# A two-layer graph network: four buffers for W1's slots, and four steps asked for in other places of the plan

## The chip, the core and the metric

The kernel runs on one core of a Trainium2 chip. The metric is the device time of one launch in microseconds (us). The engines go by their short names: PE (TensorE, matmuls; PEld its weight loads), DVE (VectorE), ACT (ScalarE), POOL (GpSimd) and SP (SyncE, which here issues nearly all transfers, in order).

## What is computed

Two graph layers over 32 graphs ("batches") of 512 nodes with 512 features, all in float32. The reference, cut to its core:

```python
# layer 0, per batch
h   = relu(layernorm(x))
agg = (adj @ h) / maximum(sum(adj, -1), 1e-6)
x   = x + relu(concat([h, agg]) @ W.T)            # W: 512 x 1024
# layer 1
h   = relu(layernorm(x))
q, k = split(h @ Wqk); v = h @ Wv
agg = adj @ (k * mask)
w   = mask * sum(q * agg, -1) / sqrt(512)
x   = x + softmax(w)[:, None] * v
```

## The kernel before

**Strassen-like products.** Each product of two 512 x 512 matrices is split into 2 x 2 blocks of 256 and done with seven block products instead of eight. A matrix that takes part is held in seven "slots" (`[P, 7, 2, H]` with P = 128, H = 256): four blocks and three sums of them. `left_sums` and `right_sums` make the sums on DVE, four operations each. `product` (L118) runs the seven products in the order 1, 2, 6, 5, 7, 3, 4. It keeps three PSUM banks: `pp` (reused by five of the products), `pr` and `pq`. After a product the result goes out of PSUM, by a copy on ACT (`c11`, `c12`, `m5`, `c22`) or by an addition on DVE (`finish`). A product that reuses a bank waits for the copy out of it.

**Stages of a batch i.** They are written as Python generators that yield between groups of matmuls:

- Y (`layer0_y`, 7 steps): h times the second half of W.
- O (`layer0_out`, 14 steps): h times the first half of W (W1), then adj times Y, added in the same banks; the output adds to x.
- TV (`layer1_tv`, 14 steps): the second layer's two products with Wq Wk^T and Wv, kept as `ptv` banks and the tile `tv`, with one more level of splitting. It runs for batch i-1 behind O of batch i. The last batches run it in two separate halves (`layer1_one`, banks `pw`).
- U (`layer1_u`, 7 steps): adj times the masked h of layer 1.

The order in time is O(i), TV(i-1), U(i), Y(i+1), O(i+1), and so on. `start` does the first batch's Y and O with its own plan, and prepares the weights.

**The plan.** Everything that isn't a matmul of the running stage is put by hand at a step of it: `p.at(n, f)` calls f after the n-th group of matmuls has been written into PE's stream. `run` emits the stage and the plan together. Since every engine takes its instructions in order, this fixes the order on all of them. Code that a stage runs behind a yield, as a copy out of a bank, comes behind what the plan put at that step.

**The parts that the plan moves about.**

- `Stream` (L402): W1's seven slots are read from DRAM again in every batch, in the order of their use, into a ring of three buffers (`tag="w1"`, tile `w`, source `dw`). Three loads are put at step 0 of U, four at steps 1, 3, 5, 7 of O.
- `FrontH`: x of a later batch into two half tiles (tile `n`, two buffers, shared with adj's half tiles `a`), its statistics on DVE, the normalisation on ACT (`write`, which also sends it to DRAM, `dhT`), the reading back in blocks (`to.read`, tile `shT`) and the 32 x 32 transposition on DVE (`turn`, tile `wide`).
- `FrontA`: the same for adj: `sum` on ACT gives the row sums (`deg`), `degrees` on DVE their reciprocals, `write` on ACT scales the rows, `daT` and `saT` are its copies, `turn` writes `aT`.
- `FrontH1` and `Post`: the second layer's front (`h1m`, `dh1T`, `sh1T`, `h1T`), and its end: `recombine` and `dot` on DVE, the softmax over nodes (`scores`, `maximum` on POOL, `shift`, `exponents` on ACT, `row_sum`, `weights`), and `apply` on ACT, which scales the rows of `tv`.

The softmax of batch 30, the last but one, is in the plan of U of batch 31: `shift` and `exponents` at step 2, behind the turns and sums of `h1T`.

The identity matrix for PE's transposes is a constant tile of its own (L218). The mask is kept twice, once with the factor 1/sqrt(512) (`mcol`, used by `factor` at L339) and once without (`mraw`).

Of the kernel before, what the change touches and what calls it, by code (L numbers as in the profile page):

```python
# [11 lines left out]
F32 = mybir.dt.float32  # L12
AF = mybir.ActivationFunctionType
ALU = mybir.AluOpType
AX = mybir.AxisListType

P = 128
# [5 lines left out]
def kernel(  # L23
# [35 lines left out]
    nc = tc.nc  # L59
    B, N, F = x.shape  # L60
    C = N // P
    H = F // 2
# [3 lines left out]
    scale = 1.0 / math.sqrt(wqk.shape[1] // 2)  # L66

    const = ctx.enter_context(tc.tile_pool(name="const", bufs=1))
    big = ctx.enter_context(tc.tile_pool(name="big", bufs=1))
# [29 lines left out]
    def copy(o, i):  # L99
        nc.scalar.activation(o, i, AF.Copy)  # L100
# [114 lines left out]

    mhalf = const.tile([P, C], F32, name="mhalf")
    nc.vector.memset(mhalf, -0.5)
    identity = const.tile([P, P], F32, name="identity")  # L218
    make_identity(nc, identity)

    X, AT_, DEG, W, Y, H1M, H1T, U, TV = ({} for _ in range(9))

    def xu_tile(name):
        return big.tile([P, C * 512], F32, tag="xu", bufs=2, name=name)

    def load_x(b):
# [87 lines left out]
    class FrontA:  # L314
# [21 lines left out]

        def factor(self):
            W[self.b] = small.tile([P, C], F32, tag="wd", bufs=3, name=f"wd_{self.b}")
            nc.gpsimd.tensor_tensor(W[self.b], DEG[self.b], mcol[:, :, self.b], op=ALU.mult)  # L339

        def write(self, c):
            v = self.n[c // 2][:, c % 2, :]
# [59 lines left out]
    class Stream:  # L402
# [6 lines left out]

        def load(self):  # L410
            k = ORDER[self.n % 7]
            t = big.tile([P, 2, H], F32, tag="w1", bufs=3, name=f"w1_{self.n}")
            nc.sync.dma_start(out=t, in_=self.d[RIGHT[k]])
            self.tiles.append((k, t))
            self.n += 1
# [281 lines left out]
        else:  # L697
            nc.vector.transpose(dst[:, :, ts(h, H)].rearrange("p a (k r) -> p k a r", r=R), t)

    mcol = const.tile([P, C, B], F32, name="mcol")  # L700
    mraw = const.tile([P, C, B], F32, name="mraw")

    def in_order(t):
# [6 lines left out]
    held = {}  # L710

    def turn_chunk(src, c, name):

        p = held[name, c] = mm_tile(f"{name}_{c}").rearrange("p a f -> p (a f)")
        for k in range(C):
            nc.tensor.transpose(p[:, ts(k, P)], src[:, ts(k, P)], identity)

    def keep_chunk(dst, c, name, by=copy):
        by(
# [4 lines left out]
    FH, FA, F1 = {}, {}, {}  # L724
# [24 lines left out]

    def start():  # L750

        load_x(0)
        s2 = [exchange(weight_source(w0[:, F:2 * F])[8 * h:8 * h + 8], f"sw2_{h}") for h in range(2)]
        fa = FA[0] = FrontA(0)
# [9 lines left out]
        fh = FH[1] = FrontH(1)  # L764
# [1 line left out]
            fh.load(h, room[:, 9728 + 1024 * h:9728 + 1024 * (h + 1)].rearrange("p (c f) -> p c f", c=2))  # L766
        sq = exchange(weight_source(wqk[:, 0:F]), "swq", rows16(5632))
        sk = exchange(weight_source(wqk[:, F:2 * F]), "swk", rows16(7680))
        late = big.tile([P, 7, 7, P], F32, tag="h1T", bufs=1, name="late").rearrange("p s i f -> p (s i f)")
        wqT = late[:, 0:2048].rearrange("p (c f) -> p c f", c=C)  # L770
        wkT = late[:, 2048:4096].rearrange("p (c f) -> p c f", c=C)
        mask_sb, mask_by = late[:B, 4096:4608], late[:B, 4608:5120]
# [4 lines left out]
        t = norm_tiles("0_0")  # L777
# [31 lines left out]
        p = Plan()  # L809
# [22 lines left out]
        fb = FA[1] = FrontA(1)  # L832
        p = Plan()
# [13 lines left out]
        p.at(7, lambda: nc.sync.dma_start(out=stream.d.rearrange("s p b f -> p s (b f)"), in_=w1R.rearrange("p s b f -> p s (b f)")))  # L847
        for h in range(2):
            for c in range(2):
                p.at(7 + 3 * h + c, fb.sum, 2 * h + c)  # L850
                p.at([11, 12, 13, 13][2 * h + c], fb.write, 2 * h + c)
            p.at(9 + 3 * h, fb.degrees, h)
        p.at(7, turn_rows, sq[:, 0:8], 0, wqT, True)
        p.at(8, turn_rows, sq[:, 8:16], 1, wqT, True)
        p.at(9, turn_rows, sk[:, 0:8], 0, wkT, False)
# [10 lines left out]
                nc.tensor.transpose(m[:, c, :], mask_by[:, ts(c, P)], identity[:B, :B])  # L866

        def mask_keep():
            nc.scalar.activation(mcol, held["pmk"], AF.Copy, scale=scale)
            nc.scalar.activation(mraw, held["pmk"], AF.Copy)  # L870

        p.at(8, mask_order)
        f = F1[0] = FrontH1(0)
# [7 lines left out]
        p = Plan()  # L881
# [7 lines left out]
                )  # L889

        def place(d, which, src):
            copy(
                mv[:, 2 * (d // 2):2 * (d // 2) + 2, 2 * (d % 2):2 * (d % 2) + 2, which, :],
                src.rearrange("p (a b f) -> p a b f", a=2, b=2),
            )

        def outer(s):
# [31 lines left out]
    with tc.manual_schedule(engines=engines):  # L929
        weights, mvR = start()  # L930
        post = None
        for i in range(B):
# [3 lines left out]
            f = F1[i]  # L936
            if i > 0:

                p = Plan()
                for n in range(4):  # L940
                    p.at(2 * n + 1, stream.load)
                right_y = right_sums(of(Y[i]))
                p.at(0, right_y[0])
# [27 lines left out]
                    p.at(2 + k, f1.inner_sums, k, 0, 7)  # L971
                if 1 < i and i + 2 < B:
                    fh = FH[i + 2]
                    for c in range(C):
                        p.at(3 + c, fh.stats, c)
                        p.at(10 + c, fh.write, c)
                    p.at(7, variance, fh.t)
                    p.at(9, shift, fh.t)
                if more:
                    th = FH[i + 1]  # L980
                    p.at(2, th.to.read, 1)
                    p.at(11, th.turn, 0)
                if 1 < i and i + 2 < B:
                    fa = FA[i + 2] = FrontA(i + 2)
# [7 lines left out]
                post = Post(i - 1, F1[i - 1])  # L992
                p = Plan()
# [19 lines left out]
                if i == 1:  # L1013
# [3 lines left out]
                    fh = FH[3]  # L1017
# [29 lines left out]
            p = Plan()  # L1047
            if more:
                p.at(0, f.turn, 0)
                p.at(1, f.turn, 1)  # L1050
                p.at(2, FA[i + 1].to.read, 0)
                p.at(3, FA[i + 1].to.read, 1)
                for n in range(3):
                    p.at(0, stream.load)
            if i == 0:
                fh = FH[2]
                for c in range(C):
                    p.at(2 + c, fh.stats, c)
                p.at(5, variance, fh.t)
                p.at(6, shift, fh.t)  # L1060
                p.at(6, weights[0])
            elif more:
                for k in range(7):
                    p.at(1 + k // 4, post.recombine, k, 1, 0)
                for c in range(C):
                    p.at(3 + c // 2, post.dot, c)
                p.at(5, post.scores)
                p.at(5, post.maximum)
                if i == 1:
                    for c in range(C):  # L1070
                        p.at(3 + c, fa.sum, c)
                    p.at(5, fa.degrees, 0)
                elif i + 2 < B:
                    for c in range(C):
                        p.at(c, fa.write, c)
                if 1 < i and i + 3 < B:
                    FH[i + 3] = FrontH(i + 3)
                    p.at(6, FH[i + 3].load, 0)
            else:
                p.at(0, f.turn, 0)  # L1080
                p.at(1, f.turn, 1)
                s4 = big.tile([P, 8, P], F32, tag="s", bufs=2, name="s4")
                for k in range(4):
                    p.at(1, f.inner_sums, k, 0, 2, s4)
                for k in range(4):
                    p.at(2 + k // 2, f.sums, k)
                for k in range(4):
                    p.at(4 + k // 2, f.inner_sums, k, 2, 7, s4)
                p.at(2, post.shift)
                p.at(2, post.exponents)  # L1090
                p.at(3, post.row_sum)
                p.at(4, post.weights)
            run(layer1_u(i), 7, p)


            if more:
                p = Plan()
                fb = FA[i + 1]
                p.at(2, fb.turn, 0)
                p.at(3, fb.turn, 1)  # L1100
                p.at(4, fb.sums, 0)
                p.at(4, fb.sums, 2)
                p.at(1, load_x, i + 1)
                if i + 2 < B:
                    p.at(5, FH[i + 2].to.read, 0)
                if i > 0:
                    p.at(0, post.shift)
                    p.at(1, post.exponents)
                    p.at(2, post.row_sum)
                    p.at(4, post.weights)  # L1110
                    for k in range(7):
                        p.at(3 + k // 2, post.recombine, k, None, 1)
                p.at(2, FA[i].factor)
                if i == 0:
                    for c in range(C):
                        p.at([2, 3, 4, 4][c], fh.write, c)
                    for k in range(1, 4):
                        p.at(3 + k, weights[k])
                    FA[2] = FrontA(2)
                    p.at(5, FA[2].load, 0)  # L1120
                    p.at(6, FA[2].load, 1)
                elif i == 1:
                    p.at(0, fa.degrees, 1)
                    for c in range(C):
                        p.at(2 + c, fa.write, c)
                    FH[4] = FrontH(4)
                    p.at(5, FH[4].load, 0)
                    p.at(6, FH[4].load, 1)
                elif i + 3 < B:
                    p.at(0, FH[i + 3].load, 1)  # L1130
                run(layer0_y(i + 1), 7, p)

        final = Post(B - 1, F1[B - 1])
        p = Plan()
# [16 lines left out]
        p = Plan()  # L1151
# [48 lines left out]
```

## Time and profile before

| | us |
|---|---|
| median of 9 runs | 2281.8 |
| lowest, highest | 2280.61, 2284.58 |
| the profiled execution (one of the nine) | 2284.58 |
| its span, first to last instruction | 2282.5 |
| outside its span | 2.08 |

The profile page starts with the busy time of each engine, and then shows the span in 40 equal slices, a digit being the busy share of a slice in tenths:

```profile
PE   7998999999999999999999999999999999999998
PEld 6787888888888888888888888888888888888897
DVE  6787888888888888888888888888888888888778
ACT  4454434454444454345444344443444443445323
POOL 0000000000100000000000000001000000000000
PEclk9999999999999999999999999999999999999999
DMA  9977878787778878777878787787788787877553
```

PE is full in all slices but a few at the start, and in the last one; DVE follows it closely; ACT has room. PEclk is the clock granted to TensorE in tenths of full speed, a mean over 57 us here, so a short drop doesn't show. DMA is the mean busy share of the 16 DMA engines.

The transfers that the change touches are these (what, by which engine's queue, times, size of one, median us from issue to landing):

```profile
w<-dw SPq DMA_DIRECT2D x217, 256.0 KB, 4.2
...
sh1T<-dh1T SPq DMA_DIRECT2D x256, 128.0 KB, 3.4
shT<-dhT SPq DMA_DIRECT2D x248, 128.0 KB, 4.4
...
saT<-daT SPq DMA_DIRECT2D x248, 128.0 KB, 3.3
...
n<-in_x_dram SPq DMA_DIRECT2D x240, 128.0 KB, 3.6
```

In the rows of the prediction a time stamp counts from the span's start. A row gives the start, the length, the engine, the line, the operation, what it writes and reads, and in square brackets the idle time before it and what ended that. Two rows of a pipelined engine overlap, so distances between starts are the measure. The line of a helper (L130 is the matmul of `product`, L100 the copy, L94 the addition, L97 the subtraction) stands for many uses; the names of the tiles tell them apart.

### The profile page before, as it was taken

The numbers are of one execution on the slowest core, as the hardware profiler recorded it, in microseconds if no ns is written. First come the engines' busy times: TensorE is split into PE (matmuls) and PEld (weight loads), VectorE is DVE, ScalarE is ACT, GpSimd is POOL, SyncE is SP. The second block draws the span as 40 slices with busy tenths as digits, with TensorE's granted clock in tenths as the row PEclk, the third lists the DMA queues.
The fourth block names the chain that finished last, engine by engine and source line by source line (L and its number), as shares of the span: only waits on it lengthen the run. The fifth ranks groups of instructions, "written<-read, shape, count | busy, mean of one in ns | idle before, by whom it ended". The sixth has DMA issues, their size and how long they took to land.

```text
span 2282.5 us, 32822 instructions
## 1 busy us (share of the span) xinstructions
PE 2252.7 (99%) x10526; PEld 1977.3 (87%) x10526; DVE 1924.3 (84%) x3802; ACT 1026.6 (45%) x1897; POOL 175.1 (8%) x260
## 2 busy tenths in 40 slices
PE   7998999999999999999999999999999999999998
PEld 6787888888888888888888888888888888888897
DVE  6787888888888888888888888888888888888778
ACT  4454434454444454345444344443444443445323
POOL 0000000000100000000000000001000000000000
PEclk9999999999999999999999999999999999999999
DMA  9977878787778878777878787787788787877553
GB/s 219 234 210 209 215 196 208 207 223 204 208 195 210 222 206 214 203 200 209 222 202 213 193 208 221 213 212 202 191 217 224 198 216 193 212 208 217 152 130 92
DMA packets 409771, 463.67 MB, mean 203 GB/s; under 512 B 37728, under 2 KB 271712, under 8 KB 405376
## 3 DMA queue, kind: packets, MB, share of 16 engines
q1 hardware_dynamic: 400192, 428.56, 69.3%
q0 software_dynamic: 8928, 32.51, 8.2%
q8 instruction: 83, 1.36, 0.3%
q14 instruction: 88, 0.72, 0.1%
q10 hardware_dynamic: 480, 0.52, 0.1%
HBM read 293.93 MB, written 167.51 MB: 202 GB/s over the span
## 4 chain that ended last, share of the span: by engine, by line
PE 95%; DMA 2%; DVE 2%; SPq 0%; ACT 0%; issue 0%; DVEq 0%; POOLq 0%
PE ptv L467 28%; PE pp_o L130 19%; PE pq_o L130 10%; PE pp_u L130 9%; PE pp_y L130 9%; PE pq_u L130 5%; PE pr_o L130 5%; PE pq_y L130 5%; PE pr_y L130 2%; PE pr_u L130 2%; PE pw L519 1%; DVE tv L94 1%; PE pm L886 1%; DMA a<-in_adj_dram 1%; DMA late<-in_nodemask_dram 0%; DMA room<-in_x_dram 0%
## 5 line engine op out<-in xcount | busy, mean ns | idle before, releaser
L467 PE MATMUL ptv<-mv,h1T 128*128 128x256 f32 x2940 | 639.5, 379 | 0.0
L467 PEld LDWEIGHTS ptv<-mv,h1T 128*128 128x128 f32 x2940 | 558.5, 190 | 76.1 <-DVE xu L446 0.2
L94 DVE TENSOR_TENSOR tv<-tv 128x256 f32<-128x256 f32 (+1 forms) x658 | 326.7, 509 | 13.5 <-ACT tv L100 1.5
L100 ACT ACTIVATE tv<-ptv 128x512 f32<-128x512 f32 (+1 forms) x360 | 185.3, 542 | 270.8 <-PE ptv L467 270.1
L130 PE MATMUL pp_u<-h1m,aT 128*128 128x256 f32 x1024 | 242.0, 379 | 1.5 <-ACT xu L100 1.5
L130 PE MATMUL pp_y<-wide 128*128 128x256 f32 x1024 | 243.4, 381 | 0.0
L130 PE MATMUL pp_o<-y,aT 128*128 128x256 f32 x1024 | 241.9, 379 | 0.0
L130 PE MATMUL pp_o<-w,wide 128*128 128x256 f32 x992 | 234.4, 379 | 0.8 <-ACT m_o L100 0.8
L130 PEld LDWEIGHTS pp_u<-h1m,aT 128*128 128x128 f32 x1024 | 194.4, 190 | 28.7 <-ACT xu L100 1.9
L130 PEld LDWEIGHTS pp_y<-wide 128*128 128x128 f32 x1024 | 195.3, 191 | 27.2 <-ACT y L100 0.6
L130 PEld LDWEIGHTS pp_o<-y,aT 128*128 128x128 f32 x1024 | 194.5, 190 | 26.4
L130 PEld LDWEIGHTS pp_o<-w,wide 128*128 128x128 f32 x992 | 188.4, 190 | 26.7 <-ACT m_o L100 1.1
L100 ACT ACTIVATE o<-pp_o 128x512 f32<-128x512 f32 x96 | 57.3, 596 | 297.5 <-PE pp_o L130 297.5
L100 ACT ACTIVATE y<-pp_y 128x512 f32<-128x512 f32 x128 | 76.4, 597 | 236.7 <-PE pp_y L130 236.7
L94 DVE TENSOR_TENSOR tv<-ptv,tv 128x512 f32<-128x512 f32 x240 | 140.0, 614 | 44.6 <-PE ptv L467 40.8
L97 DVE TENSOR_TENSOR h1T<-h1T 128x512 f32<-128x512 f32 (+2 forms) x193 | 165.9, 873 | 1.2
L100 ACT ACTIVATE xu<-pp_u 128x512 f32<-128x512 f32 x128 | 76.4, 597 | 195.4 <-PE pp_u L130 195.4
L248 POOL TENSOR_TENSOR rstd<-rstd,mhalf 128x2 f32<-128x2 f32 (+1 forms) x96 | 78.6, 819 | 657.8 <-DVE rstd L247 657.8
L130 PE MATMUL pq_o<-w,wide 128*128 128x256 f32 x496 | 119.3, 384 | 5.3 <-DMA w<-dw 5.1
L130 PE MATMUL pq_o<-y,aT 128*128 128x256 f32 x512 | 121.9, 381 | 0.0
L130 PE MATMUL pq_u<-h1m,aT 128*128 128x256 f32 x512 | 121.0, 379 | 0.0
L130 PE MATMUL pq_y<-wide 128*128 128x256 f32 x512 | 120.9, 379 | 0.0
(128 smaller groups left out, 3212.0 us busy)
## 6 DMA issues: line engine op xcount, KB each, us to landing
w<-dw SPq DMA_DIRECT2D x217, 256.0 KB, 4.2
xu<-in_x_dram SPq DMA_DIRECT2D x128, 256.0 KB, 5.3
a<-in_adj_dram SPq DMA_DIRECT2D x256, 128.0 KB, 3.2
dh1T<-h1m SPq DMA_DIRECT2D x128, 256.0 KB, 3.2
dx<-xu SPq DMA_DIRECT2D x32, 1024.0 KB, 4.9
sh1T<-dh1T SPq DMA_DIRECT2D x256, 128.0 KB, 3.4
shT<-dhT SPq DMA_DIRECT2D x248, 128.0 KB, 4.4
daT<-a SPq DMA_DIRECT2D x124, 256.0 KB, 3.0
```

The lines of the kernel that those rows point to most:

```text
L94: (on or nc.vector).tensor_tensor(o, a, b, op=ALU.add)
L97: (on or nc.vector).tensor_tensor(o, a, b, op=ALU.subtract)
L100: nc.scalar.activation(o, i, AF.Copy)
L130: nc.tensor.matmul(p[:, rc, :], lt[:, LEFT[k], dk, ts(rc, P)], right[:, dk, :], start=first and n == 0, stop=True, skip_group_check=True,)
L248: nc.gpsimd.tensor_tensor(rstd[:, a:b], rstd[:, a:b], mhalf[:, a:b], op=ALU.pow)
L467: nc.tensor.matmul(banks[n][:, :, ts(i, P)], left[:, LEFT[k], LEFT_IN[j], :], mvR[:, RIGHT[k], RIGHT[j], :, :], start=first and i == 0, st ...
L519: nc.tensor.matmul(banks[n][:, ts(i, P)], held[:, s, :] if held is not None and j == 3 else left[:, s, LEFT_IN[j], :], mvR[:, RIGHT[k], RI ...
L886: nc.tensor.matmul(m.rearrange("p a f -> p (a f)"), wqT[:, a, ts(d, P)], wkT[:, a, :], start=(a == 0), stop=(a == C - 1),)
```

## The change

Six things change:

1. W1's ring gets four buffers. Four loads are at step 0 of U, three at steps 1, 3, 5 of O.
2. x of batch 4 is loaded in O of batch 2 (steps 3 and 5), and no longer in Y of batch 2 (steps 5 and 6). Its statistics, variance, shift and writes stand at later steps there. The second reading of `shT` goes from step 2 of O to step 4, and in O of batch 2 to step 6.
3. In O of batch 0 the sums over adj of batch 1 come one step later; the reciprocals follow them.
4. In U of the last batch `shift`, `exponents` and `row_sum` of batch 30 are put at step 0 ahead of the turns, and `weights` at step 1 behind them.
5. The identity is made in a part of a tile that is used only at the start and shares the buffer of `h1T`.
6. `mcol` is gone: `factor` uses `mraw`, and the factor 1/sqrt(512) goes into the copy that puts Wq Wk^T in place (`place`, `which` = 0).

```diff
-    identity = const.tile([P, P], F32, name="identity")
-    make_identity(nc, identity)
...
-            nc.gpsimd.tensor_tensor(W[self.b], DEG[self.b], mcol[:, :, self.b], op=ALU.mult)
+            nc.gpsimd.tensor_tensor(W[self.b], DEG[self.b], mraw[:, :, self.b], op=ALU.mult)
...
-            t = big.tile([P, 2, H], F32, tag="w1", bufs=3, name=f"w1_{self.n}")
+            t = big.tile([P, 2, H], F32, tag="w1", bufs=4, name=f"w1_{self.n}")
...
-    mcol = const.tile([P, C, B], F32, name="mcol")
...
+        late = big.tile([P, 7, 7, P], F32, tag="h1T", bufs=1, name="late").rearrange("p s i f -> p (s i f)")
+        identity = held["identity"] = late[:, 5120:5248]
+        make_identity(nc, identity)
         load_x(0)
...
-                p.at(7 + 3 * h + c, fb.sum, 2 * h + c)
+                p.at(8 + 3 * h + c, fb.sum, 2 * h + c)
                 p.at([11, 12, 13, 13][2 * h + c], fb.write, 2 * h + c)
-            p.at(9 + 3 * h, fb.degrees, h)
+            p.at(10 + 2 * h, fb.degrees, h)
...
-            nc.scalar.activation(mcol, held["pmk"], AF.Copy, scale=scale)
-            nc.scalar.activation(mraw, held["pmk"], AF.Copy)
+            copy(mraw, held["pmk"])
...
-            copy(
+            nc.scalar.activation(
                 mv[:, 2 * (d // 2):2 * (d // 2) + 2, 2 * (d % 2):2 * (d % 2) + 2, which, :],
-                src.rearrange("p (a b f) -> p a b f", a=2, b=2),
+                src.rearrange("p (a b f) -> p a b f", a=2, b=2), AF.Copy, scale=1.0 if which else scale,
             )
...
-                for n in range(4):
+                for n in range(3):
                     p.at(2 * n + 1, stream.load)
...
                     fh = FH[i + 2]
+                    late = i == 2
+                    if late:
+                        p.at(3, fh.load, 0)
+                        p.at(5, fh.load, 1)
                     for c in range(C):
-                        p.at(3 + c, fh.stats, c)
-                        p.at(10 + c, fh.write, c)
-                    p.at(7, variance, fh.t)
-                    p.at(9, shift, fh.t)
+                        p.at((6 if late else 3) + c, fh.stats, c)
+                        p.at([11, 12, 13, 13][c] if late else 10 + c, fh.write, c)
+                    p.at(9 if late else 7, variance, fh.t)
+                    p.at(10 if late else 9, shift, fh.t)
                 if more:
                     th = FH[i + 1]
-                    p.at(2, th.to.read, 1)
+                    p.at(6 if i == 2 else 4, th.to.read, 1)
...
-                for n in range(3):
+                for n in range(4):
                     p.at(0, stream.load)
...
             else:
+                p.at(0, post.shift)
+                p.at(0, post.exponents)
+                p.at(0, post.row_sum)
                 p.at(0, f.turn, 0)
                 p.at(1, f.turn, 1)
+                p.at(1, post.weights)
...
-                p.at(2, post.shift)
-                p.at(2, post.exponents)
-                p.at(3, post.row_sum)
-                p.at(4, post.weights)
...
-                    p.at(5, FH[4].load, 0)
-                    p.at(6, FH[4].load, 1)
```

More of the change, by code (lines that the diff above doesn't have):

```diff
@@ L715, in turn_chunk @@
         for k in range(C):
-            nc.tensor.transpose(p[:, ts(k, P)], src[:, ts(k, P)], identity)
+            nc.tensor.transpose(p[:, ts(k, P)], src[:, ts(k, P)], held["identity"])
     def keep_chunk(dst, c, name, by=copy):
@@ L768, in start @@
         sk = exchange(weight_source(wqk[:, F:2 * F]), "swk", rows16(7680))
-        late = big.tile([P, 7, 7, P], F32, tag="h1T", bufs=1, name="late").rearrange("p s i f -> p (s i f)")
         wqT = late[:, 0:2048].rearrange("p (c f) -> p c f", c=C)
```

## The prediction

> **What bounds the kernel now.** I read the busy shares first, then the chain that ended last, then TensorE's waits, then the order of time around the largest of them.
>
> ```profile
> PE 2252.7 (99%) x10526; PEld 1977.3 (87%) x10526; DVE 1924.3 (84%) x3802; ACT 1026.6 (45%) x1897; POOL 175.1 (8%) x260
> ```
>
> TensorE (PE) works 99% of the span, so only its remaining gaps can be won. The chain (start, length, what) shows where they are:
>
> ```profile
> 120.17 21.21 PE ptv L467 x98
> ...
> 198.98 21.15 PE ptv L467 x98
> ...
> 268.48 21.15 PE ptv L467 x98
> ```
>
> A batch is 322 matmuls (TV 98, U 56, Y 56, O 112). 98 of them take 21.15 us, 0.2158 each, so 322 need 69.50. From 198.98 to 268.48 is exactly 69.50: the steady state has no gap, and no edit can shorten it. From 120.17 to 198.98 is 78.81, 9.31 too long. TensorE's waits (us in total, times, longest) name the reason:
>
> ```profile
> PE h L716 <- ACT h L788: 13.4, 1, 13.4
> PE pq_o L130 <- DMA w<-dw: 5.1, 1, 5.1
> PE pp_u L130 <- ACT xu L100: 1.5, 1, 1.5
> PE pp_o L130 <- ACT m_o L100: 0.8, 1, 0.8
> PE pw L519 <- DVE tv L94: 0.7, 1, 0.7
> PE pq_o L130 <- ACT m_o L100: 0.4, 1, 0.4
> ```
>
> The first is the start, which the change leaves alone. The second is O of batch 2, seen in TensorE's timeline:
>
> ```profile
> 174.24 1.89 PE L130 MATMUL pp_o<-y,aT 128*128 128x256 f32 x8
> 181.22 3.75 PE L130 MATMUL pq_o<-w,wide 128*128 128x256 f32 x8 [5.08 <-DMA w<-dw]
> 184.76 2.87 PE L130 MATMUL pq_o<-y,aT 128*128 128x256 f32 x8
> 188.38 1.97 PE L130 MATMUL pp_o<-w,wide 128*128 128x256 f32 x8 [0.75 <-ACT m_o L100]
> ```
>
> Groups of eight that follow each other at 1.73 suddenly lie 3.54 and 3.62 apart. The windows (length, busy of PE, PEld, DVE, ACT, POOL, then granted clock, DMA share, GB/s) say why:
>
> ```profile
> 171.00:176.00 5.00, 5.00 (x24) 4.18 (x22) 4.93 (x9) 1.95 (x3) 2.06 (x2) 1.00 0.81 183
> 176.00:181.00 5.00, 0.13 (x1) 0.00 (x0) 4.93 (x9) 0.60 (x1) 0.00 (x0) 0.89 0.99 203
> 181.00:186.00 5.00, 4.78 (x11) 3.87 (x12) 4.93 (x9) 0.00 (x0) 0.00 (x0) 0.50 1.09 226
> 186.00:191.00 5.00, 4.25 (x18) 3.40 (x17) 0.85 (x4) 0.60 (x1) 1.06 (x1) 0.93 0.67 215
> ```
>
> After the gap the clock stands at 0.50. O of batch 2 runs from 165.61 to 198.81, 33.20, where 112 x 0.2158 = 24.17 would do: **9.03 lost**.
>
> **Part by part.** *Fourth W1 buffer, x of batch 4 into O.* SP issued eight x transfers at 168.93 (5.40 us, held by the adj copies that still read the buffers), and the fourth W1 slot came behind them at 174.43 and landed 6.65 later. Now that slot is asked for in U of batch 1 (SP's W1 row at 151.39), 25 us before its matmul at 175.97. The other three go out at steps 1, 3, 5 of O (about 168.9, 171.1, 174.5) for matmuls at 179.4, 182.9, 186.3, with the x transfers behind the second and third and the second shT read behind those (176.7, for a turn in TV step 3 after 194); W1 lands in 4.2 (median), so 5 us are spare. The adj copies that held the x buffers have landed by 171, so SP does not stand there either. The idle 5.25, the slow clock (16 matmuls in 6.41 instead of 3.45) and the 0.75 behind it go.
>
> Here a rule and a row differ. The Trainium skill, "TensorE: Matmul & The Clock Gate", Part 1, has the gate at half rate after an idle window of about 3.4 us, and open again after about 3.4 us of work: that costs 1.7. The row has 2.96 beyond the pause. By the rule the place is worth 5.25 + 1.7 + 0.75 = 7.7, by the rows 9.03; I take the rows. The rule agrees with the trace on what matters next: a short wait doesn't drop the clock (after the 1.51 in U the groups run at full speed).
>
> *What is late next there.* DVE is behind in this O: it began late because the transposed adj came late,
>
> ```profile
> 163.07 1.25 DVE L280 STREAM_TRANSPOSE aT<-saT 128x1024 f32<-128x1024 f32 x1 [1.34 <-DMA saT<-daT]
> ```
>
> and it was still busy while TensorE stood. Its work to the end of batch 4's statistics is the same in another order and ends as now at 186.6. From o<-m_o to the end of xu<-pp_o batch 3 needs 6.62 (262.58 to 269.2); with the shift moved between, 186.7 + 6.62 + 0.08 = 193.4. TV's fourth bank of its second product waits for that; TensorE gets there at 165.61 + 24.17 + 19 x 0.2158 = 193.88. Slack 0.5. The added W1 transfer goes ahead of the saT reads on the queue and pushes them. Bounds: one more issue, 0.4; or 256 KiB at the 213 GB/s of the stretch 157 to 161, 1.23. The skill ("DMA: Bandwidth & Descriptors", Issuing engines are not separate DMA queues) says that all DMAs interleave on the same 16 engines, which speaks against the move; by its 435 GB/s it would cost 0.6. I take the row less the spare share before it (0.88 busy in 153 to 157, so 0.12 x 4): 0.75. A wait of **0.25** is left: -9.03 + 0.25 = -8.8. At the lower bound it is 0, at the upper 0.7.
>
> Batch 4's x is now normalised at about 188.2 to 191, its buffer free for adj at 192.4, adj landed near 197.4; ACT's sum over it stands in TV's step 4 and holds ACT's copies behind it until 199.4, where TensorE needs them at 201.9. Hidden with 2.5 to spare; without that cover, microseconds of stall in TV.
>
> *In every batch*: one W1 slot in U rather than O, and the second shT read moved from step 2 to 4. The slot read at O's step 10 was late in batches 4 and 20 (0.36 and 0.08 over 69.50); it is now asked for two steps (3.5 us) earlier. Batch 1's fourth slot, 0.36 late at 106.12, comes in U of batch 0. Together **-0.8**. The saT reads of batch 3 landed about 233.8 and DVE turned them at 236.38 and 237.58, so 1.23 more hides; the shT read has 17 us until its turn at 273.99.
>
> *Sums over adj of batch 1 one step later.* The sum at 48.62 waited 3.16 on ACT for adj, with m_o behind it; TensorE lost 49.88 - 49.27 = 0.61 and 0.1 after. Now m_o runs at 46. Next late is the copy of c22, behind two sums, done by 51.3 for a matmul at 52.7: hidden. The two degree steps wait less. The gain can be lost again, as Y of batch 1 is held by ACT at 90.20, and the DMAs there (share 1.06 to 1.23) need not move. From 0 to 0.71; I take **-0.5**, since the x writes that start that chain move earlier too.
>
> *Softmax first in U of the last batch.* Expected to free this wait:
>
> ```profile
> 2245.36 0.30 ACT L628 ACTIVATE e<-w,ntop 128x4 f32<-128x4 f32 x1 [5.22 <-DVE ntop L625]
> ...
> 2246.19 1.99 PE L130 MATMUL pp_u<-h1m,aT 128*128 128x256 f32 x8 [1.51 <-ACT xu L100]
> ...
> 2254.55 0.72 ACT L640 ACTIVATE tv<-tv,sm 128x512 f32<-128x512 f32 x1 [0.82 <-DVE tv L94]
> ...
> 2258.69 0.58 ACT L100 ACTIVATE m_w<-pw 128x512 f32<-128x512 f32 x1
> ...
> 2259.30 0.69 DVE L94 TENSOR_TENSOR tv<-pw,m_w 128x512 f32<-128x512 f32 x1 [0.80 <-ACT m_w L100]
> ```
>
> U gains 1.77 (1.67 and 0.1). But DVE now waits for ACT's exponent before its turns: in the last softmax ntop to the end of es is 0.63. That displaces 0.07 + 0.11 (the two later) and a wait of 0.27: DVE is 0.18 later. ACT's row scales follow DVE, m_w follows them, TensorE's next products and DVE's (0.80 idle) follow m_w. So the lead of 1.77 ends at 2258.7, and the end moves by **+0.2**. From -1.8 to +0.3; I take the row that is waited for.
>
> *Identity in another tile, mcol gone, scale in the weights:* the same instructions but one copy of 0.26 on ACT, which hides under pm: 0.
>
> **Sum.** -8.8 - 0.8 - 0.5 + 0.2 = -9.9. Against the profiled execution's 2284.58 (span 2282.5): 2274.7. That execution is the longest of nine, 2.8 above the median of 2281.8. If its excess lies in the W1 wait, 2274.7 stands for all; if elsewhere, 2271.9. I take the middle, **2273.3**.
>
> **Rivals.** *The tail keeps U's gain* (0.13): the end is gated by TensorE; -1.9 more, 2271.4. For it: the gap is real; against: DVE's 0.80 wait for m_w. *A new wait in O or TV of batch 2* (0.18): DVE or ACT 3 to 5 us late, without or with the clock's drop; 2276.5 to 2279. For it: 0.5 of slack; against: idle places in TV. *W1 isn't what holds O* (0.03): another transfer comes as late; 2281. *Slower* (0.04): the extra 256 KiB ahead of saT makes DVE late in each of 29 batches. It decides from 2.6 us of delay in steady state (233.8 to 236.4); 0.6 beyond it gives 29 x 0.6 = 17.4 against -9.9: 2289. For it: the queue is full there; against: the transfer is worth 1.23. The forecast itself has 0.62, 2271.5 to 2275.5.
>
> **Numbers.** The range 2270.0 to 2277.8 takes in the tail's rival and half of the new wait. 0.2% is 4.6 us, about what can be told from no change: faster means under 2277.2. That holds for the forecast, the tail's rival and 0.11 of the new wait: 0.86; same 0.10; slower 0.04.
>
> **What would show it.** No TensorE wait on w<-dw and clock 1.00 in O of batch 2; TV of batch 1 to TV of batch 2 at 69.5 to 70; m_o without a wait near 46; U of the last batch without a gap, but a wait on m_w after it and the end no earlier relative to U's start. Wrong if O of batch 2 still loses over 2 us, or if the steady batch is not 69.50.

## The result, and the profile after

| us | before | after |
|---|---|---|
| median (runs) | 2282.94 (29) | 2274.97 (9) |
| lowest, highest | 2280.61, 2287.08 | 2274.08, 2275.55 |
| the profiled execution | 2284.58 | 2275.60 |
| its span | 2282.5 | 2273.8 |

The ratio is 0.9964, with a 95% interval of 0.9956 to 0.9973, so 0.36% is won; between the medians it is 8.0 us. The median of before takes in more runs, made beside those of after, and is 1.1 above that of the first nine. The profiled execution of after is not one of its nine runs.

The busy shares of after (TensorE 99%, DVE 85%, ACT 45%) hardly differ from before; as before they don't show the gain. TensorE's waits of after (what waited, for whom, us in total, times, longest) do:

```profile
PE h L713 <- ACT h L787: 13.5, 1, 13.5
PE pw L517 <- ACT tv L100: 1.3, 1, 1.3
PE pp_y L130 <- ACT y L100: 0.8, 1, 0.8
PE pw L517 <- DVE tv L94: 0.8, 1, 0.8
PE ptv L465 <- DVE xu L444: 0.6, 1, 0.6
PE pr_u L130 <- ACT h1m L377: 0.4, 1, 0.4
PE pw L517 <- ACT m_w L100: 0.2, 1, 0.2
```

No wait on `w<-dw` is left. The waits for `h` and for DVE's `tv` were there before; the other five, of 0.2 to 1.3, are new, each a place where another engine now comes last. O of batch 2 in TensorE's timeline of after is free of the pause (start, length, operation, groups of eight at 1.73):

```profile
173.76 1.99 PE L130 MATMUL pp_o<-y,aT 128*128 128x256 f32 x8
175.60 1.89 PE L130 MATMUL pq_o<-w,wide 128*128 128x256 f32 x8
...
189.41 5.34 PE L465 MATMUL ptv<-mv,h1T 128*128 128x256 f32 x24
195.34 5.01 PE L465 MATMUL ptv<-mv,h1T 128*128 128x256 f32 x22 [0.58 <-DVE xu L444]
```

and the windows of after from 176 on (length, busy of PE, PEld, DVE, ACT, POOL, then granted clock, DMA share, GB/s) show the clock at full speed throughout, with transfers as dense as before:

```profile
176.00:181.00 5.00, 5.00 (x25) 4.38 (x25) 4.96 (x8) 0.99 (x2) 0.00 (x0) 1.00 1.06 218
181.00:186.00 5.00, 5.00 (x25) 4.41 (x24) 4.63 (x8) 0.60 (x1) 0.00 (x0) 1.00 1.11 234
186.00:191.00 5.00, 5.00 (x25) 4.41 (x24) 3.96 (x9) 0.68 (x1) 1.36 (x1) 1.00 0.82 232
```

By the starts of the stages on TensorE, the 8.7 between the two spans come from these stretches:

| stretch | before | after | difference |
|---|---|---|---|
| start to O of batch 1 | 95.48 | 95.11 | -0.37 |
| O of batch 1 | 24.53 | 24.18 | -0.35 |
| TV of batch 0 | 21.20 | 21.55 | +0.35 |
| U of batch 1 and Y of batch 2 | 24.40 | 24.19 | -0.21 |
| O of batch 2 | 33.20 | 24.38 | -8.82 |
| TV of batch 1 to TV of batch 2 | 69.50 | 70.35 | +0.85 |
| the two batches of 69.86 and 69.58 | | 69.50 each | -0.44 |
| the last full O's end to the end of the span | 67.79 | 68.09 | +0.30 |

All other batches take 69.50 in both.

What O of batch 1 wins, TV of batch 0 gives back. At its 25th matmul the weight load waits longer for DVE's `xu` than before (before first, then after):

```profile
125.13 0.94 PEld L467 LDWEIGHTS ptv<-mv,h1T 128*128 128x128 f32 x5 [0.19 <-DVE xu L446]
124.77 1.38 PEld L465 LDWEIGHTS ptv<-mv,h1T 128*128 128x128 f32 x7 [0.54 <-DVE xu L444]
```

From O of batch 1 to U of batch 1 both traces have 45.73. DVE works there without a gap from its turns of saT to that `xu`, 33.93 in both, so the W1 slot that comes in time doesn't shorten this stretch. Eleven of the 14 traces below have 45.72 or 45.73 there, with three buffers or four.

The +0.85 in TV of batch 1 is a new wait, the 0.58 shown above. On DVE's timeline of after (in brackets the idle time before the row and what ended it):

```profile
160.96 1.25 DVE L278 STREAM_TRANSPOSE aT<-saT 128x1024 f32<-128x1024 f32 x1 [3.61 <-DMA saT<-daT]
163.72 1.25 DVE L278 STREAM_TRANSPOSE aT<-saT 128x1024 f32<-128x1024 f32 x1 [1.48 <-DMA saT<-daT]
...
186.67 0.69 DVE L240 BATCH_NORM_STATS2 st<-n 128x6 f32<-128x512 f32 x1 [0.94 <-DMA n<-in_x_dram]
...
194.60 0.69 DVE L444 SCALAR_TENSOR_TENSOR xu<-pp_o,xu 128x512 f32<-128x512 f32 x1
```

The first two rows are the turns of the transposed adj, which wait longer for saT than before. There the second wait was 1.34, and the first was

```profile
160.44 1.25 DVE L280 STREAM_TRANSPOSE aT<-saT 128x1024 f32<-128x1024 f32 x1 [2.67 <-DMA saT<-daT]
```

The third row waits for x of batch 4, which is now asked for later: a wait that before didn't have. The last row frees the bank that TensorE wants at 194.59, and ends at 195.3. TensorE's row at 195.34 shows its end, 0.58 idle and the pipeline's part, 0.75 of the 0.85.

The tail, on ACT's, TensorE's and DVE's timelines of after:

```profile
2245.84 0.72 ACT L638 ACTIVATE tv<-tv,sm 128x512 f32<-128x512 f32 x1 [2.89 <-DVE tv L94]
...
2248.37 0.72 ACT L638 ACTIVATE tv<-tv,sm 128x512 f32<-128x512 f32 x1 [1.32 <-DVE tv L94]
2249.00 0.47 ACT L100 ACTIVATE tv<-pw 128x384 f32<-128x384 f32 x1
...
2249.98 0.58 ACT L100 ACTIVATE m_w<-pw 128x512 f32<-128x512 f32 x1
```

```profile
2249.52 0.94 PE L517 MATMUL pw<-mv,h1T 128*128 128x128 f32 x6 [1.26 <-ACT tv L100]
```

```profile
2250.60 0.69 DVE L94 TENSOR_TENSOR tv<-pw,m_w 128x512 f32<-128x512 f32 x1 [0.80 <-ACT m_w L100]
```

U of batch 31 has lost its gap (12.09 instead of 13.86), but the lead is used up here: ACT stands before the row scalings (L638) until DVE has built `tv`, and the copies that TensorE and DVE need (L100) stand behind them. DVE's wait of 0.80 for `m_w` is as long as before.

### The profile page after: what moved, and what is told of

Same layout as the page of the kernel before. It is cut to its first block, busy times and chain, and to the rows that moved or that the text cites. A ratio compares the mean times of both kernels' runs of the same rounds, so it can differ in the third digit from the quotient of the medians.

```text
span 2273.8 us, 32878 instructions
## 1 busy us (share of the span) xinstructions
PE 2248.6 (99%) x10526; PEld 1974.6 (87%) x10526; DVE 1923.5 (85%) x3802; ACT 1025.8 (45%) x1896; POOL 175.8 (8%) x260
## 3 DMA queue, kind: packets, MB, share of 16 engines
q1 hardware_dynamic: 400192, 428.56, 69.7%
q8 instruction: 83, 1.36, 0.3%
## 4 chain that ended last, share of the span: by engine, by line
PE 91%; DMA 3%; DVE 3%; SPq 1%; ACT 1%; issue 0%; POOL 0%; DVEq 0%; POOLq 0%; ACTq 0%
PE ptv L465 27%; PE pp_o L130 18%; PE pp_y L130 9%; PE pp_u L130 9%; PE pq_o L130 9%; PE pq_u L130 5%; PE pq_y L130 5%; PE pr_o L130 4%; PE pr_y L130 2%; PE pr_u L130 2%; DMA n<-in_x_dram 1%; PE pw L517 1%; DVE tv L94 1%; DMA a<-in_adj_dram 0%; DMA wvN<-in_L_gnn_Wv_dram 0%; SPq L212 0%
## 5 line engine op out<-in xcount | busy, mean ns | idle before, releaser
L100 ACT ACTIVATE tv<-ptv 128x512 f32<-128x512 f32 (+1 forms) x360 | 184.6, 541 | 260.9 <-PE ptv L465 260.5
L100 ACT ACTIVATE o<-pp_o 128x512 f32<-128x512 f32 x96 | 57.3, 597 | 294.9 <-PE pp_o L130 294.9
L100 ACT ACTIVATE y<-pp_y 128x512 f32<-128x512 f32 x128 | 76.4, 597 | 233.5 <-PE pp_y L130 233.5
L100 ACT ACTIVATE xu<-pp_u 128x512 f32<-128x512 f32 x128 | 76.4, 597 | 195.7 <-PE pp_u L130 195.7
L94 DVE TENSOR_TENSOR tv<-ptv,m_tv 128x512 f32<-128x512 f32 (+1 forms) x120 | 71.9, 622 | 56.3 <-PE ptv L465 54.7
```

Of the source, the lines that this page charges most:

```text
L94: (on or nc.vector).tensor_tensor(o, a, b, op=ALU.add)
```

## The experiments

Base of each is the changed kernel, so the kernels called "alone" keep items 3 to 6 of the list of changes. Since the lengths of the start vary between executions (see the run of the changed kernel again, below), I compare stretches in the traces, and the medians only where they differ by more. "Lost" is the time from O of batch 2 to TV of batch 2 over 24.17 + 69.50 = 93.67. "Turn" is how long before O of batch 2 DVE began the second turn of saT. "Tail" is the last row of the table above. The median of the runs of before beside them was 2283.66, 2283.18 and 2282.49 in the three groups of four. The tail is given where an edit touches it; in the other kernels it is 68.05 to 68.15.

| kernel | start of O of batch 1 | O of batch 2 | lost | turn | tail | median, ratio to before |
|---|---|---|---|---|---|---|
| before | 95.48 | 33.20 | 9.03 | 2.54 | 67.79 | |
| after | 95.11 | 24.38 | 1.06 | 1.31 | 68.09 | 2274.97, 0.9964 |
| after, again | 94.81 | 24.22 | 0.31 | 1.47 | 68.04 | 2274.52, 0.9965 |
| ring alone | 95.88 | 29.17 | 4.99 | 2.59 | | 2278.98, 0.9979 |
| x alone | 95.94 | 26.76 | 3.62 | 3.55 | | 2305.20, 1.0092 |
| x alone, read kept off | 95.69 | 24.63 | 0.46 | 1.56 | | 2276.21, 0.9972 |
| fourth load late | 93.62 | 24.18 | 0.02 | 3.58 | | 2275.22, 0.9963 |
| x earlier | 95.67 | 25.00 | 0.83 | 0.90 | | 2276.10, 0.9963 |
| softmax back | 95.92 | 25.46 | 1.29 | 0.23 | 67.80 | 2276.07, 0.9968 |
| sums back | 95.56 | 24.18 | 0.07 | 1.54 | | 2275.19, 0.9965 |
| scalings later | 95.68 | 25.14 | 0.97 | 0.55 | 66.73 | 2274.01, 0.9960 |
| three together | 96.99 | 26.49 | 2.32 | 1.24 | 66.78 | 2274.21, 0.9968 |
| and softmax back | 95.81 | 24.18 | 0.00 | 2.16 | 67.56 | 2274.25, 0.9963 |
| and additions on POOL | 94.63 | 24.17 | 0.00 | 2.59 | 71.85 | 2278.49, 0.9983 |

**The ring alone.** x of batch 4 goes back to Y of batch 2.

```diff
-                    late = i == 2
+                    late = False
...
-                    p.at(6 if i == 2 else 4, th.to.read, 1)
+                    p.at(4, th.to.read, 1)
...
                     FH[4] = FrontH(4)
+                    p.at(5, FH[4].load, 0)
+                    p.at(6, FH[4].load, 1)
```

> The changed kernel with x of batch 4 put back into Y of batch 2 (steps 5, 6) and its statistics, writes and the second shT read at their usual steps; the four W1 buffers stay. Theory (the place in O of batch 2 had two causes that add up: the fourth slot asked too late, and SP held by the x transfers until 174.4): the first slot of O lands early, as now, but the second is asked for behind the x transfers at about 174.4 and lands 4.2 to 6.65 later, at 178.6 to 181 for matmuls at about 179; TensorE waits 0 to 2.2 there, without the clock falling to a half for long; O of batch 2 takes 24.4 to 27 (33.20 before, 24.38 after), the median 2274.5 to 2277.5. Rival (the ring is all that matters): no wait on w, O of batch 2 at 24.2 to 24.5, median as after, 2275. Rival (SP standing is all that matters): a wait near the old 5 comes, with the slow clock, O of batch 2 over 31, median over 2281.

The ratio is 0.9979 (0.9969 to 0.9989); O of batch 2 takes 29.17, beyond both the theory's range and the ring's rival, short of the other. SP's queue and TensorE's timeline of this run:

```profile
168.80 5.34 SPq L204 DMA_DIRECT2D n<-in_x_dram  x8
174.24 2.05 SPq L411 DMA_DIRECT2D w<-dw  x2
```

```profile
182.97 3.51 PE L130 MATMUL pp_o<-w,wide 128*128 128x256 f32 x8 [3.21 <-DMA w<-dw]
186.31 1.89 PE L130 MATMUL pp_o<-y,aT 128*128 128x256 f32 x8
```

SP stands in the x transfers for 5.34, and the W1 slots go out at 174.24 as I said, but take 8.6 and 10.2 to land instead of 4.2 to 6.65. With the wait of 3.21 the clock drops, as a window of this run shows (0.50):

```profile
184.00:186.00 2.00, 2.00 (x6) 1.64 (x5) 1.97 (x5) 0.00 (x0) 0.00 (x0) 0.50 1.22 206
```

Eight matmuls take 3.34 from start to start instead of 1.73. So the fourth buffer moves the stall by one slot and shortens it; alone it is worth 4.0 of the 8.8 in O of batch 2.

**x alone**, three W1 buffers.

```diff
-            t = big.tile([P, 2, H], F32, tag="w1", bufs=4, name=f"w1_{self.n}")
+            t = big.tile([P, 2, H], F32, tag="w1", bufs=3, name=f"w1_{self.n}")
...
-                for n in range(3):
+                for n in range(4):
                     p.at(2 * n + 1, stream.load)
...
-                for n in range(4):
+                for n in range(3):
                     p.at(0, stream.load)
```

> The changed kernel with three W1 buffers and loads as before (three in U, four in O at steps 1, 3, 5, 7); x of batch 4 stays in O of batch 2. Theory: SP doesn't stand, so the fourth slot is asked for at about 169 and lands at 173 to 175.6, for matmuls at about 175.6; O of batch 2 takes 24.2 to 24.7. In every batch the W1 transfer ahead of saT is gone; batches 4 and 20 and batch 1 have their 0.36, 0.08 and 0.36 of waits back (the batch of 4 at 69.86). Median 2274.7 to 2276. Rival (the fourth buffer is needed): a wait of 2 to 5 on w, with the clock at a half behind it, O of batch 2 27 to 33, median 2278 to 2282.

Neither: 30 us slower than after, 1.0092 (1.0078 to 1.0106). O of batch 2 is only a small part of it; the batches take 69.7 to 71.6 instead of 69.50. Its waits on TensorE begin with

```profile
PE pq_o L130 <- DMA w<-dw: 17.5, 25, 1.8
```

and SP's queue of this run in a steady batch (O starts at 308.98) shows why:

```profile
310.90 3.79 SPq L411 DMA_DIRECT2D w<-dw  x2
314.78 3.62 SPq L212 DMA_DIRECT2D shT<-dhT  x4
318.50 3.10 SPq L411 DMA_DIRECT2D w<-dw  x2
```

The second shT read, which the change put at step 4, now stands between W1 loads. The third load leaves 9.5 after O's start, together with the fourth, and they land 8.8 and 6.7 later. In before the read stood behind the first load, ahead of the other three: in the same batch there (O starts at 313.64)

```profile
315.56 0.34 SPq L413 DMA_DIRECT2D w<-dw  x1
316.00 1.86 SPq L212 DMA_DIRECT2D shT<-dhT  x4
319.01 7.23 SPq L413 DMA_DIRECT2D w<-dw  x3
```

the second load leaves 5.4 after O's start, and nothing comes between it and the last two. I had counted what the x transfers do to the queue, and forgotten the read.

**x alone, with the read kept off the W1 loads.**

```diff
-                    p.at(6 if i == 2 else 4, th.to.read, 1)
+                    p.at(8 if i == 2 else 2, th.to.read, 1)
```

> Three W1 buffers with the loads of before, x of batch 4 in O of batch 2 as after, and the second shT read back at step 2 of O, in O of batch 2 at step 8 behind the last W1 load (the run e2_x_alone had it at steps 4 and 6, ahead of W1 loads). Theory: the slow batches of e2_x_alone came from the shT read between the W1 loads: the batches go back to 69.50, those of 4 and 20 to 69.58 to 69.86; in O of batch 2 the first slot comes in time, but with three buffers the third load there waits for its slot until about 175 and shares the queue with x, so a wait of 0.5 to 1.5 stays: O of batch 2 25 to 27, median 2275.5 to 2278. Rival (moving x alone cures O of batch 2): 24.2 to 24.6 there, median under 2275.5. Rival (three buffers with x moved are slow in every batch, whatever the read does): batches of 70.2 or more, median over 2300.

The batches are back at 69.50 (one of 69.74 is left), the ratio is 0.9972 (0.9962 to 0.9983), 29 us under the run before: one read's place among the W1 loads is worth that much with three buffers. O of batch 2 takes 24.63 with a wait of 0.21, a little better than I expected: moving x, with that O's second shT read behind the last W1 load, wins 8.6 of the 8.8 with three buffers. O of batch 1 has its 0.35 back (24.52).

So the two parts are not a sum: 4.0 for the ring, 8.6 for x, 8.8 for both. What held O of batch 2 was SP standing in the x transfers; the fourth buffer adds 0.2 there and a few tenths in later batches (0.44 in the trace of before, 0.24 in this one), and allows the read at step 4. Its 0.35 in O of batch 1 comes back in TV of batch 0.

**The fourth W1 load behind the saT reads**, in U of batch 1.

```diff
-                    p.at(0, stream.load)
+                    p.at(5 if i == 1 and n == 3 else 0, stream.load)
```

> The changed kernel with the fourth W1 load in U of batch 1 at step 5, behind the saT reads, not ahead of them. Theory A (what is late in TV of batch 1 is set by the second half of x of batch 4, which lands at 186.6): saT of batch 2 turns about 1 earlier, but the statistics then wait 1.5 to 2 for x instead of 0.94, and TensorE's wait on xu in TV stays at 0.4 to 0.6; TV of batch 1 to TV of batch 2 70.2 to 70.4 (70.35 after). Theory B (my prediction: the W1 transfer ahead of saT makes DVE late): the wait on xu goes, 69.5 to 69.7, 0.7 to 0.85 off the time.

TensorE's wait goes (0.02 lost), as theory B has it. Yet DVE behaves as theory A has it: the turn begins 3.58 ahead of O, and the statistics then wait for x, on DVE's timeline of this run

```profile
183.71 0.69 DVE L240 BATCH_NORM_STATS2 st<-n 128x6 f32<-128x512 f32 x1 [2.13 <-DMA n<-in_x_dram]
```

2.13 instead of 0.94. From the first of x's four issues to this row are 11.4, in after 12.4. One trace can't say whether the load's place or this run's early start (93.62) did it; the kernels below with the same edit help.

**The second half of x one step earlier.**

```diff
-                        p.at(5, fh.load, 1)
+                        p.at(4, fh.load, 1)
```

> The changed kernel with the second half of x of batch 4 asked for at step 4 of O of batch 2, not 5, so ahead of the third W1 load there; the fourth W1 load in U is unchanged. Theory A (x is what is late): x is issued at about 172.8 instead of 174.24, the statistics' wait of 0.94 shrinks to 0 to 0.3, xu<-pp_o comes 0.6 to 0.9 earlier and TensorE's wait of 0.58 in TV goes; TV of batch 1 to TV of batch 2 69.5 to 69.8. Theory B (the W1 transfer ahead of saT): nothing changes, 70.2 to 70.4. The third W1 load comes 3 later; theory of no harm: still no wait on w.

The statistics don't wait for x any more and the wait on xu is gone, TV to TV 69.50, by theory A. No wait on w came of it here. But saT was late in this run (turn 0.90 ahead of O), TensorE waited for DVE's sums of y inside O instead, and 0.83 is lost. Both theories hold a part: what comes last of saT and x sets DVE, and where DVE is late, in O or in TV, is one loss in two places.

**The softmax back.**

```diff
-                p.at(0, post.shift)
-                p.at(0, post.exponents)
-                p.at(0, post.row_sum)
                 p.at(0, f.turn, 0)
                 p.at(1, f.turn, 1)
-                p.at(1, post.weights)
...
+                p.at(2, post.shift)
+                p.at(2, post.exponents)
+                p.at(3, post.row_sum)
+                p.at(4, post.weights)
```

> The changed kernel with shift, exponents, row_sum and weights of batch 30 back at steps 2 to 4 of U of batch 31, behind the turns. Theory (the tail is set by the chain DVE, ACT scaling, m_w, DVE): U of the last batch takes 13.9 instead of 12.1, with TensorE's wait on xu back, and all of it is made up at m_w: from the last TV's end to the end of the span the time is 0.1 to 0.3 shorter than in the changed kernel. Rival (TensorE sets the end): 1.5 to 1.8 longer.

TensorE's wait of 1.51 is back in U (13.86), and the tail is 67.80, 0.29 shorter than after. That is beyond the scatter: the eight traces with the softmax first and the rest of the tail unchanged have 68.04 to 68.15, the two with it behind the turns 67.79 and 67.80. The theory holds; as it stands, the moved softmax costs a little.

**The sums over adj of batch 1 back at their steps.**

```diff
-                p.at(8 + 3 * h + c, fb.sum, 2 * h + c)
+                p.at(7 + 3 * h + c, fb.sum, 2 * h + c)
...
-            p.at(10 + 2 * h, fb.degrees, h)
+            p.at(9 + 3 * h, fb.degrees, h)
```

> The changed kernel with the sums over adj of batch 1 (and the reciprocals) back at their old steps in O of batch 0. Theory (start is held later by ACT, at the copies of y in Y of batch 1): TensorE's wait on m_o of 0.4 to 0.6 is back near 49, but the wait on ACT's y near 90 shrinks by as much; O of batch 1 starts within 0.4 of 95.1 to 95.9, where the runs with the change have it. Rival (prediction): O of batch 1 starts 0.5 to 0.7 later than in the runs with the change, at 96 to 96.6.

The wait on m_o is back (0.32 at 49.85), TensorE doesn't wait for y near 90 at all in this run, and O of batch 1 starts at 95.56. With the sums one step later twelve executions have 93.62 to 96.99, the middle ones 95.68 and 95.69. The step gains nothing that can be seen there.

**The scalings of batch 30 later.**

```diff
-            p.at(4 + c, post.apply, c)
-        p.at(6, post.add_x1, 0)
-        p.at(8, post.add_x1, 1)
+            p.at(8 + c, post.apply, c)
+        p.at(10, post.add_x1, 0)
+        p.at(12, post.add_x1, 1)
```

> The changed kernel with the four scalings of batch 30's rows (apply) at steps 8 to 11 of the last batch's first half TV instead of 4 to 7, and add_x1 at 10 and 12. Theory (ACT stands before these rows until DVE has added them, and m_w waits behind them; DVE then waits 0.80 for m_w): ACT's copies tv and m_w are no longer held, TensorE's waits of 1.26 and 0.16 and DVE's 0.80 go, the end comes 0.6 to 1.0 earlier. Rival (DVE's work is the bound and the 0.80 is taken elsewhere): within 0.2 of the changed kernel. Rival (the last transfers wait for the later add_x1): 1 or more later.

The tail is 66.73, 1.36 shorter than after, more than expected. ACT's timeline of this run has m_w 3.5 earlier against the tail's start, and the scalings behind it:

```profile
2246.94 1.22 ACT L100 ACTIVATE m_w<-pw 128x512 f32<-128x512 f32 x2 [0.40 <-PE pw L517]
2248.06 2.72 ACT L638 ACTIVATE tv<-tv,sm 128x512 f32<-128x512 f32 x4
```

DVE's waits of 0.80 and 0.30 for m_w go; its chain then runs without a gap. The ratio is 0.9960 (0.9947 to 0.9972). The mean of its five runs is 2273.7, that of the 14 of the changed kernel 2274.9. By its trace it beats both kernels; the intervals of the ratios overlap.

**Three edits together** (fourth load late, x earlier, scalings later).

> The changed kernel with the three edits that helped in the trace together: the fourth W1 load of U of batch 1 behind the saT reads, the second half of x of batch 4 one step earlier in O of batch 2, and batch 30's scalings later in the tail. Theory (O and TV of batch 2 lose about 1 in the changed kernel, by whichever of saT and x comes last; the tail 1.36): O of batch 2 at 24.2 to 24.5 and TV to TV 69.5, the tail from the last pw of batch 30 at 66.6 to 66.9; the median 1.8 to 2.6 below the changed kernel's run beside it. Rival (e4_fourth_late had an early start by chance, and the load's place does nothing): O of batch 2 at 24.9 to 25.5, as in the runs e4b_x_earlier, e3_softmax_back and e6_apply_later; the median 1.0 to 1.6 below.

A miss in its trace: O of batch 2 takes 26.49. The x transfers now stand ahead of the third W1 load, SP spends 6.87 on them, and the load leaves at 181.03:

```profile
174.06 6.87 SPq L204 DMA_DIRECT2D n<-in_x_dram  x8
181.03 0.45 SPq L411 DMA_DIRECT2D w<-dw  x1
```

TensorE waits 1.81 for it. Of the four kernels with x earlier only this one waits for W1: its x transfers start 7.2 after O's start, those of the other three 5.75. So the step has little room, and why the queue was late here is not shown. The median (2274.21) is no better than the changed kernel's beside it (2274.52). The tail keeps its 66.78.

**The same with the softmax back.** The diffs of the two are those above.

> As e7_three_together, with the softmax of batch 30 back behind the turns in U of batch 31. Theory (in the tail DVE is now the bound, without a gap from U to the last scores): U of batch 31 takes 1.77 more, DVE's chain is 0.2 to 0.3 shorter, so the tail is 0.2 to 0.3 shorter than in e7_three_together, 66.3 to 66.6. Rival (with ACT out of the way TensorE sets the end, and the softmax's place is worth its 1.77 now): the tail 0.5 to 1.8 longer, 67.2 to 68.5.

The rival holds: the tail is 67.56, 0.78 longer than with the softmax first (66.78; 66.73 in the run of the scalings). The chain that ended last runs over TensorE's U and pw here. With ACT's scalings out of the way the moved softmax is worth 0.78; behind them it cost 0.29.

**Additions on POOL.**

```diff
-            p.at(k // 2, post.recombine, k, None, 1)
+            p.at(k // 2, post.recombine, k, None, 1, nc.gpsimd if k >= 3 else None)
...
+        for c in range(C):
+            p.at(c // 2, post.apply, c)
+        p.at(0, post.add_x1, 0)
+        p.at(1, post.add_x1, 1)
-        p.at(1, post.store, 0)
-        p.at(1, post.store, 1)
+        p.at(3, post.store, 0)
+        p.at(3, post.store, 1)
```

(`apply` and `add_x1` go out of the plan before.)

> As e7_three_together, with the last four of the seven additions that put batch 30's tv together on POOL instead of DVE, and the scalings, add_x1 and the stores behind them in the last product's plan. Theory (DVE's work is the bound of the tail): DVE is freed of 4 x 0.68 = 2.7, of which 0.4 to 1.2 shows, since TensorE's products come next; the tail 65.5 to 66.4. Rival (POOL disturbs DVE, or its additions are slow enough to hold ACT and the stores): the tail 67 or more.

The tail is the rival's, 71.85, but not for the rival's reason. POOL's four additions take 5.93, 1.48 each, and are done by 2249.2, ACT's scalings by 2253.5. But the edit also moved add_x1, which POOL issues, behind `maximum` on POOL's queue, and that waits for DVE:

```profile
2257.80 0.38 POOL L620 PARTITION_ALL_REDUCE gtop<-top  x1 [8.61 <-DVE top L617]
2258.64 1.98 POOL L645 DMA_DIRECT2D tv<-dx  x2 [0.46 <-issue]
```

So add_x1 leaves only at 2258.64, and SP's queue has batch 30's stores, which wait for it, in front of the last ones:

```profile
2264.82 5.26 SPq L670 DMA_DIRECT2D out_dram<-tv  x8
2270.27 3.10 SPq L663 DMA_DIRECT2D out_dram<-out  x6
```

What the additions on POOL are worth with add_x1 ahead of `maximum` is not tested.

**The changed kernel again.**

> The changed kernel itself again, beside the others on the same chip. If the start's length varies from run to run by chance, O of batch 1 starts anywhere from 93.6 to 96, and O of batch 2 with the batch behind it loses 0 to 1.3 over 24.17 and 69.50; the median within 2273.5 to 2276.5. If the first trace was the rule: 95.1, and 1.06 lost.

The start is 94.81 and 0.31 is lost, so both vary between executions. The five traces with this O of batch 2 (after, again, softmax back, sums back, scalings later) lose 1.06, 0.31, 1.29, 0.07 and 0.97, mean 0.74. The four with the fourth load behind saT lose 0.02, 2.32 (1.81 of it the wait on W1), 0 and 0. DVE's turn begins 0.23 to 2.59 ahead of O with the load ahead of saT (seven traces, middle 1.31), 1.24 to 3.58 with it behind (four, middle two 2.16 and 2.59), and 1.56 to 3.55 without that load (three, middle 2.54). The load's place costs DVE about 1.1, under a scatter as large. That the small loss in O of batch 2 and the TV behind it comes from it is likely, not settled.

## Why the prediction was right, and where its sum was off

The main step held. The pause, the slow clock and the wait behind them went from O of batch 2 (-8.82; the rows' 9.03 was the better guide than the 7.7 by the rule). The rival that something else holds it is refuted: with x moved and three buffers, 8.6 of it goes. The predicted time was 2273.3, the median 2274.97. Under it lay a base of 2283.2 (2273.3 + 9.9), the middle of two that couldn't be told apart; by luck it is within 0.3 of the 2282.94 of more runs. So the 1.7 is missing in the sum: 9.9 was predicted, and 8.0 lie between the medians.

Against the profiled span, where the terms can be read one by one, -8.7 was measured:

- **The wait left in TV, behind O of batch 2**, 0.25 predicted, 0.85 measured after an O that lost 0.21 (mean of both over five traces 0.74). Three sizes were off. The extra W1 load pushed saT by 1.1 to 1.23 between the two traces, my upper bound, where I took 0.75; the 0.6 estimated from the 435 GB/s of the Trainium skill ("DMA: Bandwidth & Descriptors", Specifications), which is a ceiling, was too small. "Its work to the end of batch 4's statistics ... ends as now at 186.6" failed: the statistics waited 0.94 for x, and ended at 188.4. TV to TV took 70.35, outside the 69.5 to 70 that I gave as a sign. Against these, TensorE's deadline was later than I had it: the fourth bank comes after 24 matmuls of TV, not 19 (the row of 24 above; 189.41 + 24 x 0.2158 = 194.59).
- **The start**, -0.5 predicted, -0.37 in the first trace, and nothing by the twelve traces together. The step failed where I saw the danger and gave it too little weight: ACT held Y of batch 1 near 90 until its own chain was through, and TensorE's lead went into that wait.
- **Batches 1, 4 and 20**, -0.8 predicted, -0.44 measured. The three waits on W1 went (0.35 and 0.44), but the 0.35 in O of batch 1 came back in TV of batch 0, where DVE's chain comes last. That chain was not in this term.
- **The tail**, +0.2 predicted, +0.30 measured; the softmax put back gives 0.29. The mechanism is the one that was told: ACT's scalings follow DVE, m_w follows them. Moving the scalings shows it from the other side.
- **Not in the sum**: U of batch 1 and Y of batch 2, -0.21; no run shows why.
- **Nothing slower in the steady state**: 69.50 in all full batches from batch 4 on. The slower rival's delay of saT stays hidden there. What the prediction didn't see is how near another cliff lay: the read moved from step 2 to 4 would have cost 29 us had the ring stayed at three.

## What to carry to other kernels

When a step moves on an in-order queue, write down the queue's whole order before and after: here a read of four transfers between two loads of a short ring cost 1 us in most batches, and nothing once the ring was one deeper. Two causes of one stall don't add: test each alone (4.0 and 8.6 for a stall of 8.8) before saying which was needed. A wait that goes ahead of a fully busy engine's chain can come back behind it, as the 0.35 did. If an engine's gap closes and the end doesn't move, look at what stands at the head of the next in-order engine: moving ACT's waiting scalings behind its copies turned a loss of 0.29 into a gain of 0.78.

## What the runs showed of the hardware

- **The price of a pause on TensorE is not proportional to it.** Waits of 1.51 and 1.81 left the granted clock at 1.00. A wait of 3.21 (the ring alone) cost 1.61 beyond itself: by the windows of that run the clock was at 0.50 from 182.7 to 186.1, for 3.4. One of 5.08 (before) cost 2.96 beyond itself: there the clock was at 0.50 from 179.9, 1.3 ahead of the first matmul, to 186.7, for 6.8. The Trainium skill, "TensorE: Matmul & The Clock Gate", Part 1, has about 3.4 us at half rate, so by estimate 1.7: the middle case agrees. In the long one the half clock lasted twice as long; why is not shown.
- **The first group of eight** of Y of batch 0 took 1.89 to 3.15 in the 13 executions with the new start's code. It didn't decide the time: with 1.89 O of batch 1 started at 95.11 and 94.81, with 3.15 at 94.63.
- **A transfer lands later when others were issued just ahead of it.** W1's 256 KB land in 4.1 to 4.3 (median of a run), in 8.6 and 10.2 behind eight x transfers (the ring alone), and in 8.8 and 6.7 behind four shT transfers (x alone).
